# The order of the constants in a planned kernel: twelve linear-attention layers and a gated FFN on one core

## The chip, the cores and the metric

The kernel runs on one core of a Trainium2 chip. The metric is the device time in microseconds (us) of one execution, and the median of several runs is given. PE is the matrix engine, DVE, ACT and POOL (GpSimd) are the vector, scalar and general engines, and SP is the engine that issues most of the transfers. PEld is the loading of weights into PE.

## The reference

The input is 16 sequences of 256 tokens with 128 features. Twelve layers of attention without softmax follow, with 16 heads of 8 features each, then a layer norm with a residual, a gated FFN with integer weights of 384 hidden features, and a second layer norm:

```
for i in range(12):
    q, k, v = split(x @ Wqkv[i].T + bqkv[i])
    att = einsum('bhqd,bhkd->bhqk', q, k) / sqrt(8)
    x = einsum('bhqk,bhkd->bhqd', att, v) @ Wproj[i].T + bproj[i] + x
x = layernorm(x0 + x)
gate, up = x @ wg.T / 127, x @ wu.T / 127
out = layernorm(x + (silu(gate) * up) @ wd.T / 127)
```

## The kernel before

There is no softmax, so each sequence's twelve layers can be carried in one matrix of 128 x 128 and a column of offsets. For each sequence the kernel forms the Gram matrix of its tokens once, less the part of the mean (`g0`), and then keeps a matrix `tst` (it starts as the identity, and its last columns hold the mean) that each layer multiplies from products of the weights with `tst` and `g0`. Only at the end is `tst` applied to the tokens (`xt`), in the FFN's part.

The 16 sequences form 8 pairs, `p` = 0 to 7 (`PB = 2`, `NP = 8`), and the pairs form two sets of four, `o` = 0 and 1 (`G = 4`, `NO = 2`). Each of the twelve layers runs once for each set, a half-layer. The steps, with the lines by which the profile names them:

- The token loads `load` (L266): pair 0 in two pieces, the others in one of 256 KB. The tokens lie in the tiles called `qgv`, which later hold other values.
- `prologue(p)`: the Gram matrix on PE (L341), the means out of it on DVE (L345, its negative L346, a copy into `tst` L347), a transposed broadcast of the means on PE (L351, which reads the identity), a copy of that row on DVE or ACT (L203 and L201, the two engines' lines in the helper `copy`), and `g0` on DVE (L358).
- `prep_weights(l)`: the load of a layer's weights (L288), their split into a high and a low part (L201 or L203, then the subtraction L206 on POOL), and six transfers on SP that turn rows of the output weights (L310, L311).
- `products` (L439 to L441, L447 to L449, L460), `heads` (L385, L504, L519), `projection` (L536 to L538 on PE, L543 on DVE): a half-layer's matrix products. L206 for `thl` on POOL splits the new `tst`.
- `center_tokens` (L367 on POOL makes the negative mean, L369 on ACT): tokens less their mean, needed in the FFN only.
- `ffn(p)`: L645 to L709. `hl` is the low part of the hidden values, by L206 on POOL or DVE; `ve` and `rs` (L610 and L611) are the norm's reciprocal root on POOL; L697 and L686 are on DVE; L703 is the transpose ahead of the last norm.

All steps from `prologue` on are not emitted where they are written. `plan.op` records a step with its prices in ns (one for each engine that could do it), what it reads and writes, and a priority. `Plan.run` then takes them in the order of a list scheduler: among the steps that can begin at the earliest moment, by priority less a small share of the length of the chain behind it, each on the engine where it would end first. Every step so chosen is emitted at once, under `tc.manual_schedule()`, which keeps the order of emission on every engine. The plan's clock starts with each engine free at 0, SP at 800 ns. What an SP transfer delivers is there in the plan 3000 ns after its end on SP (`AFTER`). The token loads cost 5 ns per KB in the plan, the weights' load 1300 ns, the six turning transfers together 3900 ns.

The constants are written ahead of all that as plain instructions, and outside of the manual schedule the framework's own scheduler places them between the others. They are:

- on DVE the zeros and ones (L214, L219), the copy of the identity into all of `tst` (L226), and three casts: `identb` (L248), `centerr` (L252), `id127r` (L258)
- on POOL the identity (`make_identity`: a memset and a selection in masks.py), `mhalf` (L228), the mask (L237, L240, L241), its four copies to `mask32` (L246), `center` (L251), `ones` (L254), `id127` (L257), and two memsets of `cp` (L557)
- on ACT two transfers (L231, L232) and a warm activation (L234), which reads `mhalf`
- on PE 24 matmuls with zeros (L221)

`identb`, `id127r` and `mhalf` are first read in the FFN (`mhalf` by the warm activation too), `centerr` in the last layer, `mask32` in the first `heads`.

Of the kernel before, what the change touches and what calls it, by code (L numbers as in the profile page):

```python
# [10 lines left out]
F32R = mybir.dt.float32r  # L11
BF16 = mybir.dt.bfloat16
I32 = mybir.dt.int32
AF = mybir.ActivationFunctionType
ALU = mybir.AluOpType
# [6 lines left out]
C = 128  # L22
# [6 lines left out]
QSCALE = 1.0 / 127.0  # L29
# [42 lines left out]
PE, ACT, DVE, POOL, SP = "pe", "act", "dve", "pool", "sp"  # L72
# [19 lines left out]
class Plan:  # L92
# [22 lines left out]

    def run(self):
        free = dict.fromkeys(AFTER, 0.0)
        free[SP] = 800.0
        slots = {k: [(0.0, i) for i in range(n)] for k, n in self.slots.items()}
        left = {o: len(o.deps) for o in self.ops}  # L120
        for o in reversed(self.ops):
            o.tail = min(o.costs.values()) + 300 + max((u.tail for u in o.users), default=0)
        ready = [o for o in self.ops if not left[o]]
        takes = lambda o: [v for v in o.vals if v.kind and v.slot is None]
        while ready:
            found = []
            for o in ready:
                if any(not slots[v.kind] for v in takes(o)):
                    continue
                held = max((min(slots[v.kind])[0] for v in takes(o)), default=0.0)  # L130
                best = None
                for e, c in o.costs.items():
                    t = max(free[e], held)
                    for d in o.deps:
                        wait = TO_PE if e == PE and d.engine in (ACT, DVE, POOL) else 30 if d.engine == e == PE else AFTER[d.engine]
                        t = max(t, d.end + wait)
                    if best is None or t + c < best[1]:
                        best = (t, t + c, e)
                found.append((best, o))
            assert found, "no slot is free"  # L140
            first = min(b[0] for b, _ in found)
            (_, end, e), o = min(((b, o) for b, o in found if b[0] <= first), key=lambda x: (x[1].prio - TAILW * x[1].tail, -x[1].tail, x[1].n))
            o.engine, o.end = e, end
            free[e] = end
            ready.remove(o)
            for v in takes(o):
                s = min(slots[v.kind])
                slots[v.kind].remove(s)
                v.slot = s[1]
            o.emit(e)  # L150
            for v in o.vals:
                if v.kind:
                    v.left -= 1
                    if not v.left:
                        slots[v.kind].append((max(x.end for x in v.ops) + 200, v.slot))
            for u in o.users:
                left[u] -= 1
                if not left[u]:
                    ready.append(u)
        assert all(o.end is not None for o in self.ops)  # L160
        self.span = max(free.values())
# [26 lines left out]
@with_exitstack  # L188
def linear_attention_ffn_kernel(ctx: ExitStack, tc: tile.TileContext, x, xt, wall, wq0, bias, wg, wu, wd, out):
    nc = tc.nc  # L190
    sb = ctx.enter_context(tc.tile_pool(name="sb", bufs=1))
    ps = ctx.enter_context(tc.tile_pool(name="ps", bufs=1, space=PSUM))
    new = lambda name, shape, dt=F32: sb.tile([128, *shape], dt, name=name)

    plan = Plan({"bank": 8, "raw": RAW, "weights": WSLOTS, "turned": WSLOTS})
# [28 lines left out]
    ident = new("ident", [128])  # L224
    make_identity(nc, ident)
    nc.vector.tensor_copy(tst[:, :, 0:C], ident.unsqueeze(1).to_broadcast([128, B, C]))  # L226
    mhalf = new("mhalf", [K])
    nc.gpsimd.memset(mhalf, -0.5)  # L228

# [14 lines left out]
    for g in range(G):  # L244
        rows = slice(32 * g, 32 * g + 32)
        nc.gpsimd.tensor_copy(mask32[rows, :], mask[rows, rows])  # L246
    identb = new("identb", [128], BF16)
    nc.vector.tensor_copy(identb, ident)  # L248

    center, centerr = new("center", [128]), new("centerr", [128], F32R)  # L250
    nc.gpsimd.tensor_scalar(center, ident, 1.0, -1.0 / C, ALU.mult, ALU.add)  # L251
    nc.vector.tensor_copy(centerr, center)  # L252
    ones = new("ones", [C], BF16)
    nc.gpsimd.memset(ones, 1.0)  # L254

    id127, id127r = new("id127", [128]), new("id127r", [128], F32R)
    nc.gpsimd.tensor_scalar(id127, ident, 1.0 / QSCALE, 0.0, ALU.mult, ALU.add)  # L257
    nc.vector.tensor_copy(id127r, id127)  # L258


    xts = [new(f"xt{p}", [PB * T]) for p in range(NP)]
# [1 line left out]
    vbias, vwq0, vhalf = Val(), Val(), Val()  # L263

    def load(dst, src, vs, prio, kb=256, reads=[]):
        plan.op({SP: kb * 5}, lambda e: nc.sync.dma_start(dst, src), reads, vs, prio)  # L266


    vq, vgv = [Val() for _ in range(NP)], [Val() for _ in range(NP)]
    for p in range(NP):  # L270

        for ks in [range(2), range(2, K)] if p == 0 else [range(K)]:
            rows = slice((p * K + ks[0]) * 128, (p * K + ks[-1] + 1) * 128)
            load(xtoks[p][:, ks[0] : ks[-1] + 1, 0:C], x[rows, :].rearrange("(k p) c -> p k c", p=128), [vq[p], vgv[p]] if ks[-1] == K - 1 else [vhalf], -9 + 0.01 * p - (p == 0), 64 * len(ks))
# [9 lines left out]
    def prep_weights(l):  # L284
# [28 lines left out]
        if 1 <= l <= NP:  # L313

            p = l - 1
            load(xts[p], xt[:, p * PB * T : (p + 1) * PB * T], [vx[p]], l, reads=[turned])
# [55 lines left out]
    kb, vb, vbb, qc, kvo = new("kb", [B]), new("vb", [B]), new("vbb", [B, 32]), new("qc", [B]), new("kvo", [B, 32])  # L372
# [356 lines left out]
    prep_ffn(L - 2)  # L729
    for p in range(NP):  # L730
        ffn(p, L + FOFF + FSTEP * p)
    with tc.manual_schedule():
        plan.run()


# [29 lines left out]
```

## Time and profile before

| what | value |
|---|---|
| median of 3 runs | 310.26 us (310.21 to 311.2) |
| the profiled execution | 310.28 us |
| its span in the trace | 308.5 us |
| instructions | 12891 |
| PE, PEld busy | 296.9 us (96%), 271.7 us (88%) |
| DVE, ACT, POOL busy | 232.3 us (75%), 213.6 us (69%), 134.0 us (43%) |
| moved by DMA | 15.66 MB |
| chain that ended last, by engine | PE 88%, DVE 6%, POOL 2%, ACT 1% |

The span runs from the first instruction of the program to the last in one profiled execution; some 1.8 us of the execution's time lie around it. A line of the timeline or of the chain starts with the time from the span's start and the duration, both in us. In the timeline, square brackets give the engine's idle time ahead of the instruction and what ended it. In the sums by stretch each engine has its busy us and, in brackets, its number of instructions. A POOL line's times are rough.

### The profile page before, as it was taken

What the parts mean: (1) busy time and instruction counts of PE and PEld (TensorE: products, weight loads), DVE (VectorE), ACT (ScalarE), POOL (GpSimd) and SP (SyncE); (2) the same over time, 40 slices, a digit from 0 to 9 for tenths busy, and PEclk for the clock granted to TensorE, in tenths of its full rate; (3) what the DMA queues carried; (4) which work ended last, traced back from release to release, by engine and by line L of the source; (5) the groups of instructions that cost most, each with busy time, mean ns of one, the idle gap of its engine ahead of it and who ended that gap; (6) DMA issues with size and microseconds to landing.
All of it is one profiled execution on the core that took longest, in us unless ns stands there. A gap on an engine that the chain in (4) does not pass through costs nothing.

```text
span 308.5 us, 12891 instructions
## 1 busy us (share of the span) xinstructions
PE 296.9 (96%) x5378; PEld 271.7 (88%) x5378; DVE 232.3 (75%) x701; ACT 213.6 (69%) x546; POOL 134.0 (43%) x218
## 2 busy tenths in 40 slices
PE   8899999999999999999999999999999999999970
PEld 7899999999999999999999999999999998887850
DVE  1787777777677676776767877686768798999983
ACT  2567687767777767777676676776885566657683
POOL 5337352334531345314452154422330359737781
PEclk9999999999999999999999999999999999999996
DMA  6533413112031130311202112030000000001124
GB/s 195 150 99 86 126 36 87 39 41 84 3 87 36 39 88 2 90 36 40 86 2 53 38 27 55 30 81 2 2 2 5 3 0 2 0 0 36 35 69 136
DMA packets 22506, 15.66 MB, mean 51 GB/s; under 512 B 1968, under 2 KB 19888, under 8 KB 22448
## 3 DMA queue, kind: packets, MB, share of 16 engines
q1 hardware_dynamic: 21888, 14.62, 17.4%
q8 instruction: 42, 0.69, 0.9%
q10 hardware_dynamic: 560, 0.22, 0.3%
q14 instruction: 16, 0.13, 0.1%
HBM read 8.02 MB, written 2.10 MB: 33 GB/s over the span
## 4 chain that ended last, share of the span: by engine, by line
PE 88%; DVE 6%; POOL 2%; ACT 1%; issue 1%; POOLq 0%; DVEq 0%; ACTq 0%
PE bank L460 13%; PE bank L439 8%; PE bank L519 8%; PE bank L441 7%; PE bank L440 7%; PE bank L447 5%; PE bank L504 4%; PE bank L536 4%; PE bank L537 4%; PE bank L538 4%; PE bank L448 3%; PE bank L449 3%; PE bank L682 3%; PE bank L683 3%; PE bank L666 2%; PE bank L341 2%
## 5 line engine op out<-in xcount | busy, mean ns | idle before, releaser
L206 POOL TENSOR_TENSOR thl<-tst,thl 128x260 fp32r<-128x260 f32 x88 | 64.7, 766 | 123.3 <-ACT thl L201 123.3
L201 ACT COPY qgv<-bank 128x256 f32<-128x256 f32 x169 | 59.7, 376 | 20.3 <-PE bank L449 14.0
L201 ACT COPY kv<-bank 128x512 f32<-128x512 f32 (+1 forms) x92 | 52.7, 573 | 21.1 <-PE bank L441 13.0
L439 PE MATMUL bank<-whl,thl 128*128 128x256 f32 x176 | 51.8, 294 | 0.0
L441 PE MATMUL bank<-whl,thl 128*128 128x256 f32 x176 | 49.6, 282 | 0.0
L440 PE MATMUL bank<-whl,thl 128*128 128x256 f32 x176 | 49.4, 281 | 0.0
L460 PE MATMUL bank<-kv,g 128*128 128x128 f32 x352 | 46.4, 275 | 0.0
L543 DVE TENSOR_TENSOR tst<-bank,tst 128x260 f32<-128x260 f32 x96 | 36.8, 424 | 10.7 <-PE bank L538 9.1
L460 PEld LDWEIGHTS bank<-kv,g 128*128 128x128 f32 x352 | 42.9, 191 | 0.4 <-issue 0.4
L201 ACT CAST thl<-tst 128x260 fp32r<-128x260 f32 x88 | 33.1, 410 | 14.7 <-DVE tst L543 14.6
L453 DVE TENSOR_SCALAR qgv<-bank,bcol 128x2 f32<-128x2 f32 x88 | 19.3, 221 | 26.2 <-ACT qgv L201 21.6
L439 PEld LDWEIGHTS bank<-whl,thl 128*128 128x128 f32 x176 | 33.1, 188 | 4.1 <-issue 4.0
L532 DVE TENSOR_TENSOR yhl<-bank,yhl 128x260 fp32r<-128x260 f32 x96 | 34.3, 419 | 0.6 <-ACT yhl L201 0.6
L440 PEld LDWEIGHTS bank<-whl,thl 128*128 128x128 f32 x176 | 33.2, 189 | 0.0
L441 PEld LDWEIGHTS bank<-whl,thl 128*128 128x128 f32 x176 | 33.1, 188 | 0.0
L447 PE MATMUL bank<-thl,whl 128*128 128x260 f32 x88 | 28.9, 329 | 0.0
L203 DVE CAST yhl<-bank 128x260 fp32r<-128x260 f32 (+1 forms) x49 | 19.4, 434 | 11.0 <-PE bank L519 11.0
L519 PE MATMUL bank<-qgv,gm 32*32 32x130 f32 x1536 | 26.2, 280 | 0.2 <-DVE gm L209 0.2
L448 PE MATMUL bank<-thl,whl 128*128 128x260 f32 x88 | 24.8, 282 | 0.0
L449 PE MATMUL bank<-thl,whl 128*128 128x260 f32 x88 | 24.7, 281 | 0.0
L201 ACT CAST yhl<-bank 128x260 fp32r<-128x260 f32 (+1 forms) x55 | 19.4, 401 | 5.8 <-PE bank L519 4.4
L519 PEld LDWEIGHTS bank<-qgv,gm 32*32 32x32 f32 x1536 | 17.5, 103 | 5.7 <-issue 0.5
(149 smaller groups left out, 697.7 us busy)
## 6 DMA issues: line engine op xcount, KB each, us to landing
wraw<-wall SPq DMA_DIRECT2D x12, 256.0 KB, 3.0
wpt<-whl SPq DMA_DIRECT2D x24, 96.0 KB, 2.2
xt<-xt SPq DMA_DIRECT2D x8, 256.0 KB, 3.5
qgv<-x SPq DMA_DIRECT2D x7, 256.0 KB, 5.2
out<-kv SPq DMA_DIRECT2D x7, 256.0 KB, 2.3
wpt<-whl SPq DMA_DIRECT2D x24, 64.0 KB, 2.4
wpt<-whl SPq DMA_DIRECT2D x24, 32.0 KB, 1.9
qgv<-x SPq DMA_DIRECT2D x2, 128.0 KB, 2.7
```

Of the source, the lines that this page charges most:

```text
L201: nc.scalar.copy(dst, src)
L206: (nc.vector if e == DVE else nc.gpsimd).tensor_tensor(dst, a, b, ALU.subtract)
L439: nc.tensor.matmul(o, hi[:, b, 0:C], hl(0, 1, 2), start=True, stop=False)
L440: nc.tensor.matmul(o, hi[:, b, 0:C], hl(1, 1, 2), start=False, stop=False)
L441: nc.tensor.matmul(o, lo[:, b, 0:C], hl(0, 1, 2), start=False, stop=True)
L447: nc.tensor.matmul(o, hl(0, 0), flat(hi), start=True, stop=False)
L448: nc.tensor.matmul(o, hl(0, 0), flat(lo), start=False, stop=False)
L449: nc.tensor.matmul(o, hl(1, 0), flat(hi), start=False, stop=True)
L460: nc.tensor.matmul(bank(pgv)[:, b * C : (b + 1) * C], g0[p][:, b, :], tv(b), start=True, stop=True)
L519: nc.tensor.matmul(bank(pys[r])[group(g + r), b * W : (b + 1) * W], gm[group(g), r * PB + b, :], qss[p][group(g), b, :], start=True, stop= ...
L532: plan.op({DVE: dve(PB * W)}, lambda e: nc.vector.tensor_tensor(yl, bank(py)[:, : PB * W], yh.bitcast(F32), ALU.subtract), [py, vyh[p]], [ ...
L543: plan.op({DVE: dve(PB * W)}, lambda e: nc.vector.tensor_tensor(ts, bank(pw)[:, : PB * W], ts, ALU.add), [pw], [vt[p], vc[p]], prio)
```

## The change

The manual schedule is entered at the start of the kernel, so the constants too stay in the order in which they are written on each engine, ahead of all that the plan emits. Three groups of lines move up, directly behind the copy of the identity into `tst`: `identb`, `center` with `centerr`, and `id127` with `id127r`; so POOL makes `center` and `id127` ahead of `mhalf` and the masks. The planner's clock starts later for DVE, ACT and POOL. The price of the token loads in the plan (x and xt) falls from 5 to 4 ns per KB.

```diff
     def run(self):
         free = dict.fromkeys(AFTER, 0.0)
-        free[SP] = 800.0
+        free.update({SP: 800.0, DVE: 4000.0, ACT: 3200.0, POOL: 4900.0})
...
 def linear_attention_ffn_kernel(...):
     nc = tc.nc
+    ctx.enter_context(tc.manual_schedule())
...
     make_identity(nc, ident)
     nc.vector.tensor_copy(tst[:, :, 0:C], ident.unsqueeze(1).to_broadcast([128, B, C]))
+    identb = new("identb", [128], BF16)
+    nc.vector.tensor_copy(identb, ident)
+
+    center, centerr = new("center", [128]), new("centerr", [128], F32R)
+    nc.gpsimd.tensor_scalar(center, ident, 1.0, -1.0 / C, ALU.mult, ALU.add)
+    nc.vector.tensor_copy(centerr, center)
+
+    id127, id127r = new("id127", [128]), new("id127r", [128], F32R)
+    nc.gpsimd.tensor_scalar(id127, ident, 1.0 / QSCALE, 0.0, ALU.mult, ALU.add)
+    nc.vector.tensor_copy(id127r, id127)
     mhalf = new("mhalf", [K])
     nc.gpsimd.memset(mhalf, -0.5)
...
         nc.gpsimd.tensor_copy(mask32[rows, :], mask[rows, rows])
-    identb = new("identb", [128], BF16)
-    nc.vector.tensor_copy(identb, ident)
-
-    center, centerr = new("center", [128]), new("centerr", [128], F32R)
-    nc.gpsimd.tensor_scalar(center, ident, 1.0, -1.0 / C, ALU.mult, ALU.add)
-    nc.vector.tensor_copy(centerr, center)
     ones = new("ones", [C], BF16)
     nc.gpsimd.memset(ones, 1.0)
-
-    id127, id127r = new("id127", [128]), new("id127r", [128], F32R)
-    nc.gpsimd.tensor_scalar(id127, ident, 1.0 / QSCALE, 0.0, ALU.mult, ALU.add)
-    nc.vector.tensor_copy(id127r, id127)
...
     def load(dst, src, vs, prio, kb=256, reads=[]):
-        plan.op({SP: kb * 5}, lambda e: nc.sync.dma_start(dst, src), reads, vs, prio)
+        plan.op({SP: kb * 4}, lambda e: nc.sync.dma_start(dst, src), reads, vs, prio)
...
-    with tc.manual_schedule():
-        plan.run()
+    plan.run()
```

## The prediction

> **What bounds the kernel now.** I read the busy slices of the page first, then sums by stretch, then the chain that ended last, then the order of time on DVE, POOL and PE around the constants.
>
> ```profile
> PE   8899999999999999999999999999999999999970
> DVE  1787777777677676776767877686768798999983
> ```
>
> Each digit is 7.7 us. PE is full from the third slice to the 38th. What happens on DVE there counts only if PE waits for it, so the change can act at the start and, through a changed plan, at the end.
>
> ```profile
> core 0: us, PE busy (x) PEld busy (x) DVE busy (x) ACT busy (x) POOL busy (x), PEclk, DMA share, GB/s
> 4.00:8.00 4.00, 3.80 (x22) 3.54 (x22) 0.92 (x6) 0.81 (x2) 1.07 (x6) 1.00 0.96 283
> 8.00:12.00 4.00, 3.09 (x26) 2.71 (x25) 4.00 (x20) 1.58 (x5) 1.68 (x7) 1.00 0.83 213
> 12.00:16.00 4.00, 4.00 (x118) 3.88 (x116) 2.32 (x14) 2.56 (x7) 0.82 (x6) 1.00 0.26 65
> ```
>
> From 8 to 12 us DVE is busy for 4.00 of 4.00 and PE for only 3.09; just before, DVE worked 0.92 of 4 us. The chain says which work that is:
>
> ```profile
> 7.70 0.07 DVE tmeans L346
> 7.77 1.14 DVE tst L226
> 8.90 0.17 DVE identb L248
> 9.07 0.10 DVE centerr L252
> 9.17 0.14 DVE id127r L258
> 9.31 0.33 DVE kv L203
> ```
>
> Four constant instructions (L226, L248, L252, L258) stand in DVE's queue between tmeans of pair 1 and the copy of pair 0's mean row, 1.14 + 0.17 + 0.10 + 0.14 = 1.55 us on the chain. In order of time:
>
> ```profile
> 1.27 0.30 POOL masks.py:199 TENSOR_SCALAR_AFFINE_SELECT ident<-ident 128x128 f32<-128x128 f32 x1
> 5.73 0.16 DVE L345 TENSOR_SCALAR means<-bank 128x2 f32<-128x2 f32 x1 [4.58 <-PE bank L341]
> 5.98 0.19 POOL L367 TENSOR_SCALAR nmeans<-means 128x2 f32<-128x2 f32 x1 [1.36 <-DVE tmeans L346]
> 7.79 1.16 POOL L367 TENSOR_SCALAR nmeans<-means 128x2 f32<-128x2 f32 x1 [1.57 <-DVE means L345]
> 10.41 0.43 PE L351 MATMUL bank<-ident,means 128*128 128x128 f32 x2 [0.68 <-DVE means L345]
> 11.52 0.43 PE L351 MATMUL bank<-ident,means 128*128 128x128 f32 x2 [0.23 <-DVE means L345]
> ```
>
> The identity is ready at 1.57, and DVE then sits idle for 4.58 us before 5.73. PE waits twice for DVE's means, of pairs 2 and 3. From start to start the steps into these two L351 are 0.95 us (9.46 to 10.41) and 0.51 us (11.01 to 11.52), where the same steps without a wait take 0.11: lost 0.84 + 0.39 = 1.23 us (the records' idle times, 0.68 + 0.23 = 0.91, are shorter because a matmul's recorded end lies behind the next one's start).
>
> **The change, part by part.**
>
> DVE's constants come before the first means. They can start when the identity is there (1.57) and take 1.55 us: done by about 3.1 if nothing else holds them. centerr and id127r need POOL's center and id127, 0.30 us each, now directly behind the identity: 1.57 + 0.60 = 2.2. So the cover is 5.73 - 3.1 = 2.6 us of idle DVE. If it were gone, pair 0's means would be late one for one, and PE would feel it once the transpose that needs them (7.34) is pushed, 1.4 us later.
>
> What DVE then does: the copy of pair 0's mean row waits for its transpose (ends 7.72) and starts at about 7.80 instead of 9.22, 1.42 earlier. Behind it all is as before: means of pair 2 at 8.78 (its gram ends at 8.62, so it is there), means of pair 3 at 9.89 (gram ends 9.73). Then PE: pair 2's transposes go straight behind pair 3's gram, 9.57 instead of 10.41 (0.84 saved); L460 of pair 0 at 9.84, its operand g0 being ready at about 8.9; pair 3's transposes at 10.29 instead of 11.52 (1.23 saved in all). DVE's 1.42 exceeds PE's 1.23, so PE is the limit again. What is late next: the gram of pair 4 moves from 12.23 to 11.00, and its tokens landed at 9.16; layer 0's weights landed at 8.35 and pairs 5, 6, 7 at 10.05, 10.96 and 11.70 (the trace's landings), all in time. Nothing after that is bound to the clock on the wall: the SP transfers of the turned weights (12.27) wait for POOL's L206, which waits for pair 3's means on DVE and moves with them. Of the 1.55 us, 1.23 arrive at PE: **-1.23 us**.
>
> POOL: center and id127 (0.61 us) move ahead of the masks, and mhalf behind both. The masks end later, but the first reader of mask32 is at 18.59. The last POOL constant ends at 4.62, and the first step of the plan on POOL starts at 5.98: 1.36 us of cover. mhalf is read by ACT's warm activation, at 3.03 behind a table load that ends there; mhalf would be ready at about 2.3, so no cost.
>
> A row speaks against this: the nmeans at 7.79 took 1163 ns, the others around 193; it ran exactly under the 1217 ns copy of L226, the copy that the change moves under POOL's constants. So bound POOL's delay between 0 and 1.22 us; I take the upper end, since the rows overlap in just this way. Then the masks end at 5.84 instead of 4.62, still ahead of 5.98; center and id127 come at about 3.4, DVE's last cast ends at about 3.7 with 2.0 us to spare; the warm activation comes at about 3.6, ahead of ACT's first copy at 4.87. Cost 0 at both ends.
>
> [...]
>
> The planner's start times: SP stays at 800 and DVE 4000, ACT 3200, POOL 4900 are new. In the plan the first gram can't start before its tokens (800 + 2 x 512 + 3000 = 4824 ns with the new price) and needs some 0.9 us, so DVE and ACT have no step before about 5.7 us: these numbers bind nothing. Cost 0.
>
> The price of a token load falls from 1280 to 1024 ns for 256 KB. In the order that SP issues (five token loads of pairs 0 to 3, layer 0's weights, four more), pair 3 lands in the plan at 7.9 instead of 8.9 us and pair 7 at 13.3 instead of 15.3; on the chip at 7.49 and 11.70. So the plan becomes truer and stays on the safe side. It can order some steps anew: layer 1's weights may be issued ahead of the turned weights of layer 0, for instance, as the queue comes free earlier in the plan. With PE full from 12 us on, another order of the same PE work costs nothing by itself. Bounds from the rows: a gap like the ones above (0.39 to 0.84) might come back, or none; I take none, because PE shows none in the next 260 us of the old order.
>
> Whether the middle and the end keep their order is read from two half-layers far apart:
>
> ```profile
> 104.41:114.14 9.73, 9.73 (x219) 9.12 (x226) 7.40 (x23) 6.56 (x17) 3.38 (x5) 1.00 0.36 97
> 182.57:192.31 9.74, 9.74 (x220) 9.13 (x226) 7.41 (x23) 6.56 (x17) 3.38 (x5) 1.00 0.26 65
> ```
>
> Same counts, same busy times: the plan has fallen into a cycle, although its first half-layers (starts of L519 at 19.67, 27.52, 36.56, 47.74) were irregular. A start with other irregularities should fall into the same one, and the end, planned from that cycle, then only shifts.
>
> Sum: 310.28 (the profiled execution; span 308.5 and 1.8 around it) - 1.23 = 309.05. That execution stands 0.02 above the median, so **309.0 us**, span 307.3.
>
> **The rivals.**
>
> Slower: the end is dealt anew. The last 14 us are a chain in which POOL runs in series:
>
> ```profile
> 295.83 1.01 POOL rs L611
> 296.84 1.24 POOL hl L206
> 298.08 0.34 POOL ve L610
> ```
>
> L206 for hl may go to POOL (1.24) or DVE (0.60 on the chain at 293.59). If two subtractions that DVE does now fall to POOL ahead of the last reciprocal roots, the end grows by 2 x 1.24 = 2.48: 309.05 + 2.48 = 311.5. It decides from the second on; with one, 310.3. For: every load's price touches the plan. Against: the locked cycle.
>
> No change: a gap of the lost size opens elsewhere, or one subtraction lands on POOL: 310.3.
>
> Better: the new deal takes POOL's 1.24 out of that chain: 307.8.
>
> The change does not do what it says: DVE's casts still follow the first means. Against: the diff emits them first and keeps order. 310.3, counted with no change.
>
> **How the numbers follow.** Forecast (308.7, were all of DVE's 1.55 us to arrive, to 309.4, were only the first gap of 0.84 to close) 0.53; better 0.09; no change, partial gains included, 0.19; slower 0.19. A measurement of this kernel tells 0.3%, 0.93 us, from no change: faster is below 309.33. That gives faster 0.62, same 0.19, slower 0.19. The range runs from the better case, 307.8, to 310.6, no change plus 0.3 for the scatter of its runs (310.21 to 311.2); outside lie nearly all of the slower case and little else.
>
> **What would show it.** Right: L226, L248, L252 and L258 end before 4 us; no PE idle before the two L351; pair 4's gram near 11.0; each later L519 about 1.2 us earlier, in half-layers of 9.73; the last 30 us unchanged in order. POOL's center or id127 stretched to some 1.2 us under L226 would confirm the row against. Wrong: a PE gap between 12 and 60 us, another count in the half-layers, or another number of L206 on POOL after 285 us.

## The result, and the profile after

The changed kernel takes 311.46 us (median of 8 runs, 311.02 to 313.04). The kernel before, run beside it, takes 310.49 us (8 runs, 309.92 to 311.36). The ratio is 1.0039 [1.0022, 1.0056]: slower, by 0.97 us, where 1.23 us of gain were forecast. The profiled execution took 311.45 us, with a span of 309.7 us. Most lines of the kernel have moved down by one: L351 is now L352, L460 is L461, L504 is L505, L519 is L520, L536 to L538 are L537 to L539.

The busy slices of the page, after:

```profile
PE   6989999999999999999999999999999999999970
```

PE is full one slice earlier, and its third digit (15.5 to 23.2 us) has fallen from 9 to 8. The first digit is lower too (6 instead of 8): in this execution pair 0's Gram matmuls took 1.25 us instead of 2.06, since the full clock came at 4.02 instead of 6.89 us (from one matmul's start to the next it is 0.21 us ahead of 6.89 in the trace of before and 0.11 behind), and PE then waited 1.48 us for pair 1's tokens. The sum of the stretch from 8 to 12 us, in the columns shown before:

```profile
8.00:12.00 4.00, 4.00 (x38) 4.00 (x37) 3.29 (x17) 2.63 (x8) 1.07 (x7) 1.00 0.93 234
```

PE is now busy for 4.00 of these 4 us, where it was 3.09. The place that the prediction looked at did what the prediction said. The timelines of DVE, POOL and PE show how:

```profile
1.46 1.23 DVE L227 COPY tst<-ident 128x2048 f32<-128x2048 f32 x1 [0.30 <-POOL ident masks.py:199]
1.51 1.34 POOL L232 TENSOR_SCALAR center<-ident 128x128 f32<-128x128 f32 x1
3.30 0.23 DVE L237 CAST id127r<-id 128x128 fp32r<-128x128 f32 x1 [0.20 <-POOL mhalf L239]
5.06 0.16 DVE L346 TENSOR_SCALAR means<-bank 128x2 f32<-128x2 f32 x1 [1.53 <-PE bank L342]
...
9.69 0.38 PE L352 MATMUL bank<-ident,means 128*128 128x128 f32 x2
9.91 1.06 PE L461 MATMUL bank<-wraw,g 128*128 128x128 f32 x8
10.80 0.38 PE L352 MATMUL bank<-ident,means 128*128 128x128 f32 x2
```

DVE's last constant ends at 3.53, 1.53 us ahead of the first means. Both L352 have no bracket any more: PE did not wait. The Gram matmuls of pair 4 begin at 11.02 instead of 12.23, which is 1.21 us earlier.

The loss stands later, where PE showed no gap before. The sums from 20 to 28 us, first before, then after:

```profile
20.00:24.00 4.00, 4.00 (x145) 3.65 (x126) 3.94 (x13) 3.32 (x10) 1.61 (x2) 1.00 0.04 11
24.00:28.00 4.00, 4.00 (x107) 3.77 (x101) 2.82 (x9) 2.94 (x7) 4.00 (x9) 1.00 0.30 69
```

```profile
20.00:24.00 4.00, 3.09 (x132) 2.62 (x114) 2.95 (x11) 1.03 (x3) 2.19 (x6) 1.00 0.19 45
24.00:28.00 4.00, 3.23 (x74) 2.55 (x79) 3.20 (x8) 2.68 (x6) 3.38 (x5) 1.00 0.28 65
```

PE was never idle in these two stretches and is now idle for 0.91 and 0.77 us of them. Its timeline there, before and after:

```profile
21.80 0.37 PE L536 MATMUL bank<-yhl,whl 128*128 128x260 f32 x1
...
23.41 0.38 PE L385 MATMUL bank<-tst,wraw 128*32 128x8 f32 x24
23.62 0.76 PE L504 MATMUL bank<-qgv,wraw 128*32 128x32 f32 x64
24.31 0.39 PE L439 MATMUL bank<-whl,thl 128*128 128x256 f32 x1
```

```profile
20.95 0.38 PE L386 MATMUL bank<-tst,wraw 128*32 128x8 f32 x24
21.16 0.47 PE L505 MATMUL bank<-qgv,wraw 128*32 128x32 f32 x32
22.54 0.46 PE L505 MATMUL bank<-qgv,wraw 128*32 128x32 f32 x32 [0.91 <-issue]
22.93 0.39 PE L537 MATMUL bank<-yhl,whl 128*128 128x260 f32 x1
...
25.41 0.39 PE L442 MATMUL bank<-whl,thl 128*128 128x256 f32 x1 [0.33 <-POOL thl L207]
27.32 0.96 PE L520 MATMUL bank<-qgv,gm 32*32 32x130 f32 x56 [0.45 <-DVE gm L210]
```

Three things are to be seen. First, the heads of set 1 for layer 0 (L386 and L505) now stand ahead of set 0's projections (L537 to L539); before, they stood behind them. Second, PE stops in the middle of the 64 matmuls of L505, and "issue" says that it waits for nothing that the profile shows. Third, two waits follow: one for POOL's split of `thl` and one for DVE's `gm`. From start to start, less the usual step of the same two lines, the losses are 1.11 - 0.01 = 1.10 us (21.43 to 22.54), 0.60 - 0.12 = 0.48 us (24.81 to 25.41) and 0.73 - 0.21 = 0.52 us (26.59 to 27.32). A fourth one of 0.35 - 0.21 = 0.14 us stands at 48.99, ahead of another L520. Together that is 2.24 us.

Behind it, the old cycle returns, 1.20 us late. One half-layer as a sum by stretch, then a line of the chain that ended last:

```profile
183.71:193.44 9.73, 9.73 (x209) 9.12 (x208) 7.41 (x23) 6.56 (x17) 3.39 (x5) 1.00 0.25 64
```

```profile
298.05 1.24 POOL hl L207
```

The half-layers take 9.73 to 9.74 us as before, and POOL's three lines of before stand in the same order, each 1.21 us later. (This stretch holds exactly one half-layer, 209 matmuls; the 219 and 220 of before were counted in stretches that began 0.07 us into an L519 and so ended in the next one.) So the middle and the end are only shifted. The start of the last half-layer's L520 went from 244.59 to 245.81: -1.21 from the start of the trace and +2.43 behind it, of which the four gaps are 2.24.

### The profile page after: what moved, and what is told of

Same layout as the page of the kernel before. It is cut to its first block, busy times and chain, and to the rows that moved or that the text cites. A ratio compares the mean times of both kernels' runs of the same rounds, so it can differ in the third digit from the quotient of the medians.

```text
span 309.7 us, 12867 instructions
## 1 busy us (share of the span) xinstructions
PE 296.0 (96%) x5378; PEld 270.4 (87%) x5378; DVE 234.8 (76%) x705; ACT 211.7 (68%) x539; POOL 135.8 (44%) x221
## 4 chain that ended last, share of the span: by engine, by line
PE 84%; DVE 7%; POOL 2%; issue 2%; DMA 1%; ACT 1%; POOLq 0%; SPq 0%; DVEq 0%; ACTq 0%
PE bank L461 14%; PE bank L520 8%; PE bank L440 7%; PE bank L442 6%; PE bank L441 6%; PE bank L448 5%; PE bank L505 4%; PE bank L537 4%; PE bank L538 4%; PE bank L539 4%; PE bank L449 3%; PE bank L450 3%; PE bank L667 2%; PE bank L342 2%; PE bank L683 2%; PE bank L684 2%
## 5 line engine op out<-in xcount | busy, mean ns | idle before, releaser
L202 ACT COPY qgv<-bank 128x256 f32<-128x256 f32 x166 | 59.1, 376 | 22.9 <-PE bank L450 15.5
L461 PE MATMUL bank<-kv,g 128*128 128x128 f32 x352 | 46.4, 275 | 0.0
L461 PEld LDWEIGHTS bank<-kv,g 128*128 128x128 f32 x352 | 42.9, 191 | 0.4 <-issue 0.4
L520 PE MATMUL bank<-qgv,gm 32*32 32x130 f32 x1536 | 26.0, 280 | 0.7 <-DVE gm L210 0.6
L520 PEld LDWEIGHTS bank<-qgv,gm 32*32 32x32 f32 x1536 | 17.2, 103 | 6.6 <-DVE gm L210 0.9
```

What stands on the lines that cost most here:

```text
L202: nc.scalar.copy(dst, src)
L461: nc.tensor.matmul(bank(pgv)[:, b * C : (b + 1) * C], g0[p][:, b, :], tv(b), start=True, stop=True)
L520: nc.tensor.matmul(bank(pys[r])[group(g + r), b * W : (b + 1) * W], gm[group(g), r * PB + b, :], qss[p][group(g), b, :], start=True, stop= ...
```

## The experiments

One table holds all runs. The third column compares with the kernel before, run beside it. Single executions scatter by about 1 us, part of it at the start of the trace: pair 1's tokens land between 5.39 and 6.40 us, and PE's clock is granted in full at any time from 3.7 to 10.4 us. So the last two columns divide each trace in two: G is the start of pair 4's Gram matmuls, and R is the time from there to the first L520 of the last half-layer. R leaves the start out.

| kernel | median us (before) | ratio | G | R |
|---|---|---|---|---|
| before | 310.26 | | 12.23 | 232.36 |
| the change | 311.46 (310.49) | 1.0039 [1.0022, 1.0056] | 11.02 | 234.79 |
| e1 order kept, price 5 | 308.92 (310.21) | 0.9962 [0.9943, 0.9982] | 12.87 | 232.02 |
| e2 price 4 alone | 312.41 (310.21) | 1.0070 [1.0050, 1.0090] | 11.45 | 234.95 |
| e3 the change again | 311.04 (310.21) | 1.0036 [1.0017, 1.0055] | 10.77 | 234.89 |
| e4 order as written before, price 5 | 308.68 (310.21) | 0.9956 [0.9939, 0.9973] | 10.69 | 232.38 |
| e5 price 4, set 1 held | 310.15 (310.17) | 1.0002 [0.9979, 1.0025] | 10.36 | 233.27 |
| e6 price 4.25 | 309.23 (310.17) | 0.9976 [0.9954, 0.9998] | 10.88 | 231.91 |
| e7 four more warm matmuls | 310.72 (310.17) | 1.0024 [1.0008, 1.0040] | 11.03 | 233.67 |
| e8 six wide warm matmuls | 311.79 (310.17) | 1.0047 [1.0029, 1.0064] | 10.75 | 235.60 |
| e9 as e5 | 309.74 (310.35) | 0.9990 [0.9971, 1.0009] | 10.32 | 233.87 |
| e10 as e1 | 308.85 (310.35) | 0.9968 [0.9948, 0.9989] | 12.68 | 232.42 |
| e11 price 4 for x alone | 311.24 (310.35) | 1.0045 [1.0022, 1.0067] | 10.82 | 234.80 |
| e12 price 4 for xt alone | 308.76 (310.35) | 0.9954 [0.9938, 0.9970] | 11.06 | 232.42 |
| e13 price 4, both held | 309.67 (310.22) | 0.9989 [0.9965, 1.0013] | 10.89 | 233.08 |

In e1 and e10 the full clock came only at 10.40 and 10.36 us in the profiled execution, and so their G is late; their medians, not these two traces, say what the order is worth.

**The two parts of the change, and the order of POOL's constants (e1 to e4).** e1 is the change with the old price, and e2 is the kernel before with the new price. e4 is the kernel before with the manual schedule from the start, and nothing moved.

```diff
e1, against the change
-        plan.op({SP: kb * 4}, ...
+        plan.op({SP: kb * 5}, ...
e2, against the kernel before
-        plan.op({SP: kb * 5}, ...
+        plan.op({SP: kb * 4}, ...
e4, against the kernel before
     nc = tc.nc
+    ctx.enter_context(tc.manual_schedule())
...
-    with tc.manual_schedule():
-        plan.run()
+    plan.run()
```

> The changed kernel with the old price of the token loads (5 ns per KB): the plan's steps then stand in the order of before, and only the constants stand elsewhere. Theory A (the order of the constants gains what was forecast, and the new price's plan loses it again with three PE gaps between 21 and 28 us): the two waits of L351 on DVE's means (0.84 and 0.39 us) close, no new gap comes, time 309.0 to 309.6, ratio to before 0.995 to 0.998. Theory B (the constants' new place itself costs, by contention or by later landings): 311 to 312, ratio 1.002 to 1.005, as the whole change.

> The kernel before with the new price alone (4 ns per KB): the plan of the changed kernel, the constants placed as before. Theory A: DVE's constants still stand ahead of pair 0's mean row (1.2 us of PE gaps by 12 us) and the new plan's gaps of some 2.2 us between 21 and 28 us come on top: 312 to 313, ratio 1.005 to 1.008. Theory B: no more than noise, 310.0 to 310.8, ratio 0.999 to 1.001.

> The whole change once more, for a second trace of it. If the PE stop of 0.9 us inside L505 at 21.6 us, for which the first trace names no semaphore, belongs to the program, it is there again at the same place; if it is an accident of that run, it is gone and this run's span is some 0.9 us shorter. The landing of pair 1's tokens at 6.4 us (5.8 before) is compared in the same way. Time 311 to 312 under both theories, ratio 1.002 to 1.005.

> The kernel before with the manual schedule entered at its start and nothing moved: center and id127 behind POOL's masks, identb and the two casts last among DVE's constants. Price and plan of before. The order of the constants kept, without POOL's reordering. By the rows, POOL ends the masks at some 5 us under the 1.2 us copy of L226, id127 comes at some 5.5 to 6 us, and DVE's casts hold the first means up by 0 to 0.8 us. Theory A: as the run with price 5 to 0.5 us above it, 309.0 to 310.0; Theory B: 311 or more.

The order alone brings 1.29 us (308.92 against 310.21) and the price alone costs 2.20 us (312.41 against 310.21). The sum is +0.91; for both together +0.97 was measured, and +0.83 in e3, beside e1 and e2. In e1's trace the two waits are gone: its L352 at 11.54 and 12.21 have no bracket, and no gap stands between 21 and 28 us. e2's trace still has the old wait of L351 and also the stop, in L504, so the two parts act in different places and add up:

```profile
10.07 0.43 PE L351 MATMUL bank<-ident,means 128*128 128x128 f32 x2 [0.68 <-DVE means L345]
...
23.11 0.46 PE L504 MATMUL bank<-qgv,wraw 128*32 128x32 f32 x32 [1.06 <-issue]
```

In e3 the stop came at the same place, with 1.37 us from start to start. e4 shows that the order as it was written is as good as the new one. Its timeline, from the constants to the first means:

```profile
1.68 1.27 POOL L241 TENSOR_SCALAR_AFFINE_SELECT mask<-mask 128x128 f32<-128x128 f32 x1
...
5.36 0.54 DVE L259 CAST id127r<-id 128x128 fp32r<-128x128 f32 x1 [0.28 <-POOL id L258]
5.65 0.26 DVE L346 TENSOR_SCALAR means<-bank 128x2 f32<-128x2 f32 x1
```

Here DVE's last cast starts at 5.36, and the first means follow it at 5.65 without idle time between. The cover is gone, and the means may be some tenths late, but PE does not feel it: G is 10.69. Moving `center` and `id127` ahead of the masks buys a margin of 1.5 us, and no time that these runs show.

**Which price, and which tokens (e6, e10 to e12).** The plan takes set 1's heads early when the price is 3, 3.5 or 4 ns per KB, and late from 4.25 to 7. e6 has 4.25. e11 gives 4 only to the loads of `x` and e12 only to those of `xt`; both ran beside e10, which is e1 again.

```diff
e6
-        plan.op({SP: kb * 4}, ...
+        plan.op({SP: kb * 4.25}, ...
e11 (loads of xt have reads, those of x have none)
+        plan.op({SP: kb * (5 if reads else 4)}, ...
e12
+        plan.op({SP: kb * (4 if reads else 5)}, ...
```

> The changed kernel with a price of 4.25 ns per KB. Of the plans for prices from 3 to 7, those up to 4 take set 1's first heads ahead of set 0's projections, those from 4.25 on do not. Theory P: the price matters only through that swap, so this run is like the one with price 5: 308.5 to 309.5, no gap over 0.3 us between 10 and 200 us. Theory Q (the truer the price, the worse by degrees): nearer to price 4, 310 to 311.5.

> The constants in order with price 5 again, as the yardstick on the same chip: 308.5 to 309.3 under both theories, ratio 0.994 to 0.998.

> The changed kernel with price 4 for the tokens of the prologue alone (x), price 5 for those of the FFN (xt). The plan takes set 1's heads ahead of set 0's projections, as with price 4 for both. Theory P: like the whole change, 310.7 to 311.7, with the stop in L505 and the two gaps behind it. Theory Q (the price of the FFN's tokens matters): 308.5 to 309.5.

> The mirror: price 5 for x, price 4 for xt. The first 100 steps on PE are those of price 5, the order differs later. Theory P: 308.5 to 309.5, no gap between 21 and 28 us. Theory Q: 310.5 or more.

e6 is faster than before (its interval ends at 0.9998), and e12 too; e11 loses all (311.24 against e10's 308.85, 2.39 us). The loss comes with the price of the prologue's tokens, and from the order that it tips, not from the price as such: at 4.25, three quarters of the way from 5 to 4, it is not there. The same stretch in e12 on PE, from its timeline:

```profile
20.85 0.37 PE L537 MATMUL bank<-yhl,whl 128*128 128x260 f32 x1
22.47 0.38 PE L386 MATMUL bank<-tst,wraw 128*32 128x8 f32 x24
22.68 0.76 PE L505 MATMUL bank<-qgv,wraw 128*32 128x32 f32 x64
23.37 0.38 PE L440 MATMUL bank<-whl,thl 128*128 128x256 f32 x1
```

Projections first, then the heads, and no gap. With set 0's projections first (from 20.85 instead of 22.93), DVE gets their results 2 us earlier, and both of PE's later waits are gone.

**The swap undone at price 4 (e5, e9, e13).** One more read makes set 1's heads in layer 0 wait for set 0's last `y`, so that the projections stand first again. e13 also makes the cast of layer 2's weights wait for that `y`; in its trace the cast then stands on ACT, at 21.20.

```diff
e5, e9
-        reads = [v for _, _, rs, _, _ in more for v in rs]
+        reads = [v for _, _, rs, _, _ in more for v in rs] + ([vyl[G - 1]] if l == 0 and o == 1 else [])
e13, in prep_weights besides
-        plan.op({ACT: act(n, True), DVE: dve(n, True)}, ..., [raw], [hl], prio)
+        plan.op({ACT: act(n, True), DVE: dve(n, True)}, ..., [raw, *([vyl[G - 1]] if l == 2 else [])], [hl], prio)
```

> The whole change, price 4 included, with one more condition in the plan: the matrix products of heads for layer 0, set 1 (L386, L505) may not be taken ahead of the last low part of set 0's y. On PE the first difference from the changed kernel is then that set 0's projections (L537 to L539) stand ahead of these products again, as before. Theory P (this one swap costs the 2.2 us): none of the three gaps between 21 and 28 us, time 308.5 to 309.5, ratio 0.994 to 0.998. Theory Q (it is the new plan's other differences, more work on DVE and another order later): 310.5 to 311.5.

> The run with set 1's heads held behind set 0's projections once more, beside price 5 on the same chip: its trace had none of the three gaps and 309.25 us, but the median of its 12 runs was 310.15 with a wide scatter. Theory P (the swap is nearly all of the 2.2 us): within 0.5 us of the run with price 5 beside it, 308.5 to 309.5. Theory Q (the rest of price 4's plan costs a part that the one trace does not show): 310.0 to 310.5, about half way.

> Price 4 with set 1's heads held as in the two runs before, and layer 2's weight cast (L204 for whl) held in the plan behind set 0's low parts of y: it moves from DVE's queue ahead of the copies of y to ACT behind them, as with price 5. In the second held run that cast waited 0.24 us for its transfer and then took 1.30 us beside POOL's L207 for whl, and PE waited 1.1 us for DVE's L533. Theory D (this cast is what the held version still loses): 308.4 to 309.2, ratio 0.994 to 0.997, less scatter, and no wait of L539 on L533 over 0.4 us. Theory E (the loss of the held version lies elsewhere): 309.7 to 310.2 as before.

The three gaps are gone in all three, and R falls from 234.8 to 233.3 (e5), 233.9 (e9) and 233.1 (e13). But none comes down to the 232.4 of the old order, and the medians lie between (1.0002, 0.9990 and 0.9989), 0.8 to 1.2 us above e1 and e10. The runs missed what the theory of the swap expected. e9's timeline showed a suspect, a cast of layer 2's weights that stands on DVE ahead of `y`:

```profile
19.07 1.27 POOL L207 TENSOR_TENSOR whl<-wraw,whl 128x512 fp32r<-128x512 f32 x1 [0.64 <-DVE mb L418]
19.31 1.30 DVE L204 CAST whl<-wraw 128x512 fp32r<-128x512 f32 x1 [0.24 <-DMA wraw<-wall]
...
21.68 0.39 PE L539 MATMUL bank<-yhl,whl 128*128 128x260 f32 x1 [1.11 <-DVE yhl L533]
```

The cast ahead of it, alone and of the same size, took 0.42 us; this one took 1.30 us beside POOL's subtraction, and PE then waited 1.11 us. e13 takes that cast away from DVE. The wait of 1.1 us went (some 0.4 us of waiting for `y` stays at L539, as in e5), but the median did not move. So the cast explains e9's trace and not the rest of the loss, some 0.7 to 0.9 us by R. The traces show where most of that rest sits. In e13 it is at two smaller waits of PE:

```profile
21.34 0.39 PE L539 MATMUL bank<-yhl,whl 128*128 128x260 f32 x1 [0.20 <-DVE yhl L533]
...
26.53 0.39 PE L442 MATMUL bank<-whl,thl 128*128 128x256 f32 x1
```

From start to start PE steps into them in 0.48 and 0.29 us, where the usual step is 0.12: 0.36 + 0.17 = 0.53 of the 0.7 us. e5 has the same two, of 0.36 and 0.18 us, and the traces of the old order have neither. Why `y` and `thl` come that late in this plan, and whether these waits are all of the loss in the medians, no run shows.

**The stop inside L505 (e7, e8).** In the traces with the stop (the change, e2, e3 and e11) PE goes on 1.3 to 1.5 us after a transfer of the instruction queue has ended, so PE may have lacked instructions. e7 has four more warm matmuls ahead of all, which puts the program behind them 8 instructions later in PE's count. e8 has six wide warm matmuls instead of 24, 36 instructions fewer (a matmul and its load are two), which moves L505 the other way.

```diff
e7
-WARM = 24
+WARM = 28
e8
-    for _ in range(WARM):
-        nc.tensor.matmul(banks[7][:, :128], zero, zero, start=True, stop=True)
+    for _ in range(6):
+        nc.tensor.matmul(banks[7], zero, zero.unsqueeze(1).to_broadcast([128, 4, 128]), start=True, stop=True)
```

> The changed kernel with 28 instead of 24 matmuls of zeros at the start (L222): PE's instructions stand 8 records (a weight load and a matmul each) later in its stream; nothing else moves in order. In three traces with price 4 PE stops inside the second L505 without a semaphore, each time at the 705th record of PE and PEld, and goes on 1.33 to 1.38 us after a 16 KB transfer of the queue of kind instruction has ended. Theory F (PE has run out of instructions that were fetched): the stop is at record 705 again, so 8 records earlier in the program, and ends some 1.35 us after that transfer. Theory S (something at that place of the program): at record 713. Time 311 to 312 under both.

> The changed kernel with 6 matmuls of zeros of 512 columns instead of 24 of 128: the same time on PE at the start, but 36 records fewer. Theory F: record 705 then lies 4 records behind the last L505, so no stop inside L505; the projections (L537) begin at the end of the wait instead, and the time is within 0.6 us of the changed kernel's, a little below. Theory S: the stop stays after the 32nd record of L505, time as the changed kernel.

In e8 the stop stayed at the same instruction by count and so came 18 matmuls later in L505. Its expectation counted a matmul as one instruction and put the stop outside of L505; that was an error of mine, and the stop moved with the count all the same. The time came out above the changed kernel's, not a little below it:

```profile
20.89 0.64 PE L505 MATMUL bank<-qgv,wraw 128*32 128x32 f32 x50
23.12 0.33 PE L505 MATMUL bank<-qgv,wraw 128*32 128x32 f32 x14 [1.59 <-issue]
```

In e7 the stop stayed at the same count too, four matmuls earlier in L505, but it shrank to a step of 0.23 us, too short for a line of its own, and the next L537 started at 22.10:

```profile
21.19 0.98 PE L505 MATMUL bank<-qgv,wraw 128*32 128x32 f32 x64
```

The stop is 0.87 us shorter than the 1.10 of the changed kernel, the other gaps stayed as they were, and R fell by 1.12 us. So in this trace the stop is on the path and costs about its length (R differs by 0.4 us between e1 and e10, two traces of one kernel). e7's median fell less, to 1.0024 against e3's 1.0036, and the two intervals overlap; 310.72 also missed the 311 to 312 that was expected. Its ten runs lie in two groups, 310.4 to 310.8 and 311.2 to 311.6; whether the stop is longer in the second is left open.

## Why the prediction was wrong

**The failed step is the price of the token loads.** The prediction said that "with PE full from 12 us on, another order of the same PE work costs nothing by itself", put bounds of "a gap like the ones above (0.39 to 0.84)" or none, and took none. It measured +2.20 (e2), +2.12 (e3 less e1) and +2.39 us (e11 less e10). The reason given, that PE shows no gap in the old order, says only that the old order feeds PE well. It says nothing of another order of the same steps. What came in place of nothing: at price 4 the planner takes set 1's heads ahead of set 0's projections; PE then stops inside those heads and later waits for POOL's `thl` and DVE's `gm`. The bound failed too: it allowed for one gap, and four came. The largest (1.10) is of a kind that the trace of before does not show. The plan is "truer" for the tokens, as the prediction said; that did not make it a better order at 21 us. Putting the projections first again takes back 1.5 to 1.7 us of the 2.43 in R (e5, e13; 0.9 in e9), and by the medians e9 takes back 1.50 of the 2.39 us between e10 and e11, which ran beside it. So the swap is some two thirds of the loss; most of the rest shows as two smaller waits of PE, and their cause is open.

**The constants were right, in place and size.** -1.23 was worked out; G moved by 1.21, and the medians by 1.29 (e1), 1.50 (e10) and 1.53 us (e4). Without the new price the forecast of 309.0 us would have held (308.92 and 308.85). Pair 4's Gram at 11.02 is the "near 11.0" of the prediction, but that it fits to 0.02 is partly luck: in this trace the first transposes began 0.12 us later than before (7.46 against 7.34), and 1.33 us were saved from there; in the other traces G lies from 10.32 to 12.87.

**POOL beside the copy was right.** `center` took 1.34 us under the 1.23 us copy, against 0.30 before. The upper end was the right one to take, but the cover that was worked out for it (5.84 against 5.98) did not hold: the last POOL constant ends at 6.19, and the first planned POOL step starts at 6.27 instead of 5.98. It cost nothing all the same, as that step's result is needed in the FFN only. e4 shows the same with another instruction: the mask selection L241 took 1.27 us (1.68 to 2.95) beside the copy (1.45 to 2.69), and the next one, L242, 0.40 us behind it.

**The planner's start times bind nothing**, as the prediction said: PE's matmuls and loads have the same order in e1 with them, in e4 without them and in the kernel before.

**The locked cycle was right.** A start with other irregularities fell into the same half-layers of 9.73 to 9.74 us, and the end only shifted.

**The slower rival had the time (311.5) and not the cause.** It dealt the end anew; the end kept its order. The true mechanism stands in the prediction in outline only: as the rival of no change, "a gap of the lost size opens elsewhere", at 310.3 us, and as a sign of error, "a PE gap between 12 and 60 us".

**A version that beats both** is the order without the new price for the prologue's tokens: e1 and e10, e4, or e12, at 308.7 to 308.9 us.

## What to carry to other kernels

In a planned kernel a price is not a small edit. A price lowered by 20%, nearer to the measured landings, can swap two steps, and the trace of the old order does not show what the new one meets; before costing such an edit at nothing, list which steps change places and what each engine behind them then gets late. A full engine is not proof of slack in its order. And when a change has parts that act in different places, run each alone: here a gain of 1.3 us and a loss of 2.2 us showed as one small loss.

## What the runs showed of the hardware that was not expected

PE seems to have run out of instructions: where it stopped, the profile names no wait. That is an estimate from the counts that follow; no record of the traces says it. The transfers of the changed kernel by queue:

```profile
q8 instruction: 42, 0.69, 1.0%
```

The columns are packets, MB and share. One packet is 0.69 MB / 42 = 16.4 KB. PE has 10852 recorded instructions (5378 matmuls, as many loads, 96 others), 258 for each of these packets. Counted in the traces, every stop inside L505 (L504 in e2) stood behind PE's instruction 705. Smaller ones inside L520, of 0.25 to 0.43 us, stood behind 6849 in four traces (the change, e5, e10, e11), which is 24 x 256 later. In the changed kernel's trace the last packet to end ahead of the second stop (at 163.62 us) is the 24th after the last one ahead of the first (at 21.16). So, as an estimate, one packet brings 256 of PE's instructions. PE went on 1.2 to 1.5 us after such a transfer ended. At 705 the stop follows how fast the 256 instructions up to there run (the stop is given from start to start):

| instructions 449 to 705 take | stop behind them | kernels |
|---|---|---|
| 2.23 us | 1.79 us | e8 |
| 2.70 us | 1.09 to 1.37 us | the change, e2, e3, e11 |
| 3.27 us | 0.23 us | e7 |
| 4.14 to 5.38 us | none | the nine others |

Run and stop together take 3.5 to 4.1 us here. That is no general limit: the 256 instructions from 4033 on ran in 3.24 to 3.26 us in all traces but e8's, and no stop followed. The 256 ahead of those had taken 7.6 to 8.0 us, those ahead of 449 at most 5.5, so a supply that gets ahead while PE is slower would fit; no run tests that. In the swapped order L520 (64 matmuls), L386 (24) and L505 (64) follow each other with little between, each matmul with its load: 2.70 us for the 256 instructions up to the stop, where the old order's trace has 4.14. By the estimate these small tiles outran the supply.

After e8's stop the granted clock fell. One sum by stretch of e8:

```profile
23.59:27.00 3.41, 3.41 (x17) 3.41 (x17) 2.30 (x6) 1.54 (x4) 1.70 (x3) 0.50 0.36 84
```

For 3.41 us PE had half its clock (the column behind POOL's count), and the step from one projection matmul to the next was 0.21 us instead of 0.12. So a stop of 1.79 us was followed by half speed, and stops of 1.09 to 1.37 us were not.
